# Moving work between engines in a two-layer graph-attention kernel: the adjacency mask, the inverse norms, the projections, and the writes of q and k in chunks

## The chip, the cores and the metric

The kernel runs on one core of a Trainium2 chip. The metric is the device time of one execution in microseconds. The core's engines each have an instruction stream of their own and wait for one another through semaphores: TensorE (PE, with its weight loads as PEld), VectorE (DVE), ScalarE (ACT), GpSimd (POOL) and SyncE (SP). In this kernel SP issues all transfers, which 16 DMA engines carry out.

## The reference

The inputs are `x` (3327 x 128) and a 0/1 adjacency `adj` (3327 x 3327, with ones on its diagonal). Two layers follow one another, and each ends in a residual and a layer norm.

```
# layer 0
norm2  = norm(x, axis=1)
cos    = beta * (x @ x.T) / (norm2 @ norm2.T + 1e-7)
P      = softmax(cos + (1 - adj) * -1e9)
x      = layernorm(x + P @ x)
# layer 1: 128 "d" groups of 8 features each
q, k, v = (x @ W.T).reshape(128, n, 8)   for Wq, Wk, Wv
a      = softmax(einsum('dnh,dmh->dnm', q, k) * 128**-0.5 + adj + adj)
out    = einsum('dnm,dmh->dnh', a, v).reshape(n, 1024) @ Wo.T
x      = layernorm(x + out)
```

The adjacency enters twice: as a mask in layer 0, and as an additive term (adj + adj) in layer 1, where the kernel needs it transposed.

## The kernel before

The 3327 nodes are padded to 3328 = 26 tiles (T) of 128 rows. There are four stages.

**Layer 0** (lines 175 to 447) runs in rounds t = -2 ... 27 of eight eighths k = 0 ... 7. The order of instructions on PE, ACT, DVE and POOL is the order in which the program calls them (`manual_schedule`); the order of transfers on SP is set by the framework's planner. A round works on several tiles at once:

- tile t: `scores` (L244), four pieces of 832 columns, at k = 0, 0, 2, 4. Each is two matmuls on PE (L190), a multiplication by the inverse norms `y` on DVE (L250) and an addition of the mask with a running minimum on DVE (L253).
- tile t+1: the inverse norms. `inverse_log` and `inverse_exp` (L228, L231) on ACT at k = 0 give a first estimate 1/(a+b) of `y`; `inverse_product` and `inverse_newton` (L236, L242) on DVE at k = 6 make one Newton step over all 3328 columns.
- tile t+2: `adj_chunk` (L209), seven chunks: up to four transposes on PE (L166) of the raw adjacency, a cast to bf16 on ACT (L215), and after the last chunk a write to `aT_s` in DRAM. At k = 7 `mask` (L221) turns the raw rows into (adj - 1) * 1e9 in place, on POOL.
- tile t+3: `load` (L199) at k = 5.
- tile t-1: `weights` (L269), two halves of Exp on ACT at k = 0; then at k = 1 ... 7 a chunk of `turn_weights` each (four transposes on PE, L166, and a copy out of PSUM on DVE, L280), followed one eighth later by `weigh0` (L288) on PE.
- tile t-2: `norm_begin`, `norm_root`, `norm_end` (DVE, ACT, DVE), `project_turn` at k = 3 (a transpose, and a copy to `x1T` on ACT, L332), and six halves of `project` (a matmul on PE, L342, and a copy to `row` on ACT, L343) at k = 4, 5, 5, 6, 7, 7. PSUM for `project` has one buffer, so a half's matmul waits for the copy of the half before it. Each second half issues the write of `row` to `q_s`, `k_s` or `v_s`.

**The preparation** (lines 746 to 804) has eight groups of 16 d. For k and for q, `prepare` loads a group (`nat`, 128 x 16 x 208, runs of 832 bytes), lets POOL reorder it into `by_t` (L754), turns it in seven chunks on PE, and splits each chunk into a high part (ACT, L765) and a low part (DVE, L766), which collect in two tiles of 3328 columns; a whole tile is then written to `kp_s` or `qp_s` in DRAM (L772). `prepare_values` does the like for v without the turn: `vals`, four sets of four d, is one tile and one write to `vt_s` (L786). From group 2 on, the first row maxima of the attention (`first_max`) run between. The tiles of units 0 and 1 are loaded after group 0.

**The steps** (lines 806 to 912) run over 288 units (a block of three query tiles times four d) of 26 steps each. A step uses `aT` (the adjacency of a block, turned, bf16) on PE (L633), and `eT` = exp(2 aT) on POOL (L860). The 26 tiles of `aT` of block 0 are loaded (`load_adj_tile`, L478) and turned into `eT` (`exp_adj_tile`, L485, on ACT) before the first step; those of later blocks within the steps. `aT`, `eT` and their pool `at_fix` are made after the preparation's pools are closed.

**The end** (lines 915 to 949) projects with Wo and makes the last layer norm.

Of the kernel before, what the change touches and what calls it, by code (L numbers as in the profile page):

```python
# [10 lines left out]
F32 = mybir.dt.float32  # L11
F32R = mybir.dt.float32r
# [7 lines left out]
P = 128  # L20
# [4 lines left out]
H = 8  # L25
# [21 lines left out]
def gnn_two_layers(  # L47
# [127 lines left out]
    with ExitStack() as l0:  # L175
# [42 lines left out]

        def mask(t: int):
            u = tiles[t]  # L220
            nc.gpsimd.tensor_scalar(u.raw, u.raw, -1.0, 1.0e9, op0=ALU.add, op1=ALU.mult)  # L221

# [4 lines left out]
            u.y = work.tile([P, NP], F32, name="y")  # L227
            nc.scalar.activation(u.y, norm_k, AF.Ln, bias=norm_c[:, t : t + 1])  # L228

        def inverse_exp(t: int):  # L230
            nc.scalar.activation(tiles[t].y, tiles[t].y, AF.Exp, scale=-1.0)  # L231

        def inverse_product(t: int):
            u = tiles[t]
            u.n = one_n.tile([P, NP], F32, name="n")
            nc.vector.scalar_tensor_tensor(  # L236
                u.n, norm_k, norm_c[:, t : t + 1], u.y, op0=ALU.add, op1=ALU.mult
            )

        def inverse_newton(t: int):  # L240
            u = tiles[t]
            nc.vector.scalar_tensor_tensor(u.y, u.n, -2.0, u.y, op0=ALU.add, op1=ALU.mult)  # L242

        def scores(t: int, j: int):  # L244
            u = tiles[t]
# [18 lines left out]
        def weights(t: int, i: int):  # L264
            u = tiles[t]
            if i == 0:
                u.den = small.tile([P, 2], F32, name="den0")
            part = u.s[:, i * half : (i + 1) * half]
            nc.scalar.activation(  # L269
                part, part, AF.Exp, bias=u.mn[:, NPC - 1 : NPC], scale=-1.0,  # L270
                accum_out=u.den[:, i : i + 1],
            )

        def turn_weights(t: int, c: int):
            u = tiles[t]
            if c == 0:
                u.pts = {}
            tp, a, b = turn(ps_tp, lambda k: u.s[:, k * P : (k + 1) * P], c)
            u.pts[c] = ptp.tile([P, 4, P], F32, name="pt")[:, : b - a, :], a, b
            nc.vector.tensor_copy(u.pts[c][0], tp)  # L280

        def weigh0(t: int, c: int):
            u = tiles[t]
# [65 lines left out]
        with tc.manual_schedule(  # L349
# [20 lines left out]
            )  # L370
            ones = const.tile([P, P], F32, name="ones")
            nc.gpsimd.memset(ones, 1.0)
            for t in range(3):
                load(t)
            ws = []
# [27 lines left out]
                nc.scalar.activation(piece(norm_k, j), score_piece(ones, sqT, j), AF.Sqrt)  # L403
            nc.scalar.preload_act_table_set("natural_log_exp_and_others")

            for t in range(-2, T + 2):

                def there(n: int):
                    return 0 <= n < T

                for k in range(8):
                    if k == 0 and there(t - 2):
                        norm_begin(t - 2)
                    if k == 0 and there(t - 1):
                        weights(t - 1, 0)
                        weights(t - 1, 1)
                    if k == 0 and there(t - 2):
                        norm_root(t - 2)
                    if there(t):
                        for i in {0: (0, 1), 2: (2,), 4: (3,)}.get(k, ()):  # L420
                            scores(t, i)
                    if k == 0 and there(t + 1):
                        inverse_log(t + 1)
                        inverse_exp(t + 1)
                    if k == 1 and there(t - 2):
                        norm_end(t - 2)
                    if k > 0 and there(t - 1):
                        turn_weights(t - 1, k - 1)
                        if k > 1:
                            weigh0(t - 1, k - 2)  # L430
                    if k == 3 and there(t - 2):
                        project_turn(t - 2)
                    if there(t + 2):
                        for i in {3: (0, 1), 4: (2,), 5: (3, 4), 6: (5,), 7: (6,)}.get(k, ()):
                            adj_chunk(t + 2, i)
                    if k == 5 and there(t + 3) and t >= 0:
                        load(t + 3)
                    if there(t - 2):
                        for i in {4: (0,), 5: (1, 2), 6: (3,), 7: (4, 5)}.get(k, ()):
                            project(t - 2, i)  # L440
                    if k == 6 and there(t + 1):
                        inverse_product(t + 1)
                        inverse_newton(t + 1)
                    if k == 7 and there(t + 2):
                        mask(t + 2)
                if there(t - 1):
                    weigh0(t - 1, NCH - 1)

# [6 lines left out]

    with ExitStack() as at:
        keys = at.enter_context(tc.tile_pool(name="at_k", bufs=3))
        sm = at.enter_context(tc.tile_pool(name="at_sm", bufs=2))
        ps_m = at.enter_context(tc.tile_pool(name="at_m", bufs=1, space=PSUM))

# [4 lines left out]
        for i in range(2):  # L465
            three = sm.tile([P, QT, 4, 32], BF16, name=f"parts{i}", bufs=1)
            nc.vector.memset(three, 0.0)
            parts.append(three)

        units = [(b, g) for b in range(NB) for g in range(G4)]  # L470
        NU = len(units)
# [246 lines left out]
        with tc.manual_schedule(  # L718
# [27 lines left out]
            with ExitStack() as pr:  # L746
# [3 lines left out]
                def prepare(g, src, dst):  # L750
                    nat = work.tile([P, HG, T * H], F32, name="nat")
                    nc.sync.dma_start(nat, heads(src)[g])
                    by_t = work.tile([P, T, P], F32, name="by_t")
                    nc.gpsimd.tensor_copy(  # L754
                        by_t.rearrange("p t (g h) -> p g t h", h=H),
                        nat.rearrange("p g (t h) -> p g t h", h=H),
                    )

                    high = work.tile([P, NP], F32R, name="high")
                    low = work.tile([P, NP], F32R, name="low")  # L760
                    for c in range(NCH):
                        tp, a, b = turn(ps_tp, lambda t: by_t[:, t], c)
                        cols = slice(a * P, b * P)
                        tp = tp.rearrange("p t k -> p (t k)")
                        nc.scalar.copy(high[:, cols], tp)  # L765
                        nc.vector.tensor_sub(low[:, cols], tp, high[:, cols].bitcast(F32))  # L766

                    for i, part in enumerate((high, low)):
                        nc.vector.tensor_copy(
                            part[:, NP - 1 : NP], part[:, NP - 1 - P : NP - P].bitcast(F32)  # L770
                        )
                        nc.sync.dma_start(  # L772
                            dst[g * HG : (g + 1) * HG, :, i].rearrange("d f n -> (d f) n"),
                            part.bitcast(F32),
                        )

                def prepare_values(g):
                    nat = work.tile([P, HG, T * H], F32, name="nat")
                    nc.sync.dma_start(nat, heads(v_s)[g])
                    vals = work.tile([P, HG, T, H + 1], F32, name="vals", bufs=1)  # L780
                    nc.gpsimd.memset(vals[:, :, :, H : H + 1], 1.0)
                    nc.gpsimd.tensor_copy(
                        vals[:, :, :, :H], nat.rearrange("p g (t h) -> p g t h", h=H)
                    )
                    nc.vector.tensor_scalar_mul(vals[:, :, T - 1], vals[:, :, T - 1], real)
                    nc.sync.dma_start(  # L786
                        vt_s[4 * g : 4 * g + 4].rearrange("a p h t f -> p a (h t f)"),
                        vals.rearrange("p (a h) t f -> p a (h t f)", a=4),
                    )

                k = 0
                for g in range(NG):
# [13 lines left out]
            fix = at.enter_context(tc.tile_pool(name="at_fix", bufs=1))  # L806
# [15 lines left out]
            aT = fix.tile([P, T, QB], BF16, name="aT1")  # L822
            eT = fix.tile([P, T, QB], F32, name="eT1")
            for j in range(T):
                load_adj_tile(0, j)

            def new_a():
                return [ps_a.tile([P, 512], F32, name="ea") for _ in range(2)]

# [4 lines left out]
            for j in range(T):  # L834
                exp_adj_tile(0, j)

            todo = []
            turn = []
# [149 lines left out]
```

## Time and profile before

Three runs took 16069.47, 16071.52 and 16073.84 us; the median is 16071.52. The profile is of one more execution:

| what | value |
|---|---|
| the profiled execution's own time | 16069.72 us |
| its span, first to last instruction | 16067.9 us |
| mean granted TensorE clock | 0.983 |
| busy: PE | 15521.0 us (97%) |
| busy: DVE | 13964.9 us (87%) |
| busy: ACT | 12606.0 us (78%) |
| busy: POOL | 13681.2 us (85%) |
| layer 0, to the last row of `v_s` issued | 0 to 1004.9 us |
| preparation, first `nat` load to the last landing | 1007.6 to 1316 us |
| steps, first to last | 1317 to 15951 us |
| end | to 16067.9 us |

How to read it: a group of instructions is named by line, engine, operation and what it writes and reads; "idle before" is the time for which its engine stood still just ahead of it, with what ended that; the chain of waits is followed back from the last instruction to what released each step. Shares of busy time are averages over stages with different limits, so each stage is read by itself. TensorE records two entries for one f32 matmul.

### The profile page before, as it was taken

To read this page: it belongs to the slowest core of one execution; us is meant where nothing else is said; L and a number is where in the kernel's file an instruction comes from. 1 tells how busy PE (TensorE), PEld (TensorE's weight loads), DVE (VectorE), ACT (ScalarE), POOL (GpSimd) and SP (SyncE) were. 2 spreads that over 40 slices of the span, in tenths; PEclk is the share of its full clock that TensorE was granted. 3 is DMA by queue.
4 is the path that set the end of the run, shared out by engine and by line. 5 is a ranking of instruction groups with operands and counts; after the bars stand their busy time and mean duration, and the time that the engine had idled before them with its cause. 6 is when DMAs were issued, how large, how long until landed. Compare 5 with 4: busy or idle time off the path is not lost.

```text
span 16067.9 us, 507030 instructions
## 1 busy us (share of the span) xinstructions
PE 15521.0 (97%) x217532; PEld 6936.2 (43%) x217532; DVE 13964.9 (87%) x16269; ACT 12606.0 (78%) x24826; POOL 13681.2 (85%) x9030
## 2 busy tenths in 40 slices
PE   6757999999999999999999999999999999999999
PEld 4543444444444444444444444444444444444555
DVE  6647999999999999999999999999999999998775
ACT  4426888888888888888888888888888888888776
POOL 1016999999999999999999999999999999998886
PEclk8878999999999999999999999999999999999999
DMA  3364111111111111111111111111111111111112
GB/s 128 117 231 145 45 50 51 54 47 51 51 51 50 51 46 55 51 51 45 57 50 45 49 53 54 44 50 51 51 50 51 50 52 51 51 45 60 61 61 75
DMA packets 483008, 995.72 MB, mean 62 GB/s; under 512 B 280274, under 2 KB 377424, under 8 KB 436208
## 3 DMA queue, kind: packets, MB, share of 16 engines
q1 hardware_dynamic: 480752, 963.28, 17.7%
q8 instruction: 1704, 27.92, 0.7%
q14 instruction: 552, 4.52, 0.1%
HBM read 813.16 MB, written 149.94 MB: 60 GB/s over the span
## 4 chain that ended last, share of the span: by engine, by line
PE 92%; DVE 5%; DMA 1%; ACT 0%; issue 0%; POOL 0%; SPq 0%; DVEq 0%; POOLq 0%; ACTq 0%
PE acc L663 28%; PE ea L633 20%; PE m L554 15%; PE eb L646 12%; PE ea L646 9%; PE eb L652 2%; PE ea L652 2%; DVE mx L569 1%; PE ea L619 1%; DVE y L242 1%; PE tp L166 1%; PE acc L288 1%; PE sc L190 1%; PE ea L681 1%; DVE mx L590 1%; DVE n L236 1%
## 5 line engine op out<-in xcount | busy, mean ns | idle before, releaser
L860 POOL TENSOR_TENSOR pb<-pb,eT 128x768 f32<-128x768 f32 (+1 forms) x7488 | 13186.4, 1767 | 1099.4 <-ACT pb L859 838.0
L569 DVE TENSOR_REDUCE mx<-m 128x2 f32<-128x1024 f32 x6784 | 8271.8, 1219 | 500.0 <-PE eb L652 278.6
L859 ACT ACTIVATE pb<-eb 128x768 f32<-128x768 f32 (+1 forms) x7488 | 5900.9, 788 | 2501.7 <-PE eb L652 1893.0
L554 PE MATMUL m<-kx,qx 32*128 32x512 f32 (+1 forms) x23296 | 6768.4, 470 | 56.1 <-DVE mx L569 49.3
L889 ACT ACTIVATE pa<-ea 128x384 f32<-128x384 f32 (+1 forms) x14976 | 6336.9, 477 | 53.5 <-PE ea L633 40.0
L663 PE MATMUL acc<-pa,vt 128*9 128x384 f32 (+1 forms) x29952 | 5902.5, 474 | 0.0
L663 PE MATMUL acc<-pb,vt 128*9 128x384 f32 (+1 forms) x29952 | 5900.5, 474 | 0.1
L590 DVE TENSOR_REDUCE mx<-m 128x1 f32<-128x512 f32 x6400 | 4377.5, 684 | 694.1 <-PE m L554 319.6
L646 PEld LDWEIGHTS <-one 3*128 3x128 bf16 x29952 | 1516.1, 91 | 5557.9 <-issue 4662.1
L633 PE MATMUL ea<-aT,two 128*32 128x384 bf16 (+1 forms) x59904 | 3714.8, 325 | 0.0
L652 PE MATMUL eb<-qx,kx 32*128 32x384 f32 (+1 forms) x14976 | 3473.2, 454 | 0.0
L652 PE MATMUL ea<-qx,kx 32*128 32x384 f32 (+1 forms) x14976 | 3443.6, 437 | 0.0
L646 PE MATMUL ea<-cx,one 3*128 3x384 bf16 (+1 forms) x14976 | 3297.9, 322 | 1.3
L554 PEld LDWEIGHTS m<-kx,qx 32*128 32x128 f32 x23296 | 2809.2, 182 | 404.1 <-DVE mx L569 97.4
L646 PE MATMUL eb<-cx,one 3*128 3x384 bf16 (+1 forms) x14976 | 2465.0, 326 | 15.2 <-ACT pb L859 14.4
L663 PEld LDWEIGHTS acc<-pa,vt 128*9 128x9 f32 x29952 | 1414.5, 91 | 784.5 <-issue 0.3
L633 PEld LDWEIGHTS <-two 128*32 128x32 bf16 x59904 | 945.3, 94 | 1420.2 <-issue 1280.9
L652 PEld LDWEIGHTS eb<-qx,kx 32*128 32x128 f32 x14976 | 1462.9, 189 | 0.0
L652 PEld LDWEIGHTS ea<-qx,kx 32*128 32x128 f32 x14976 | 1434.6, 182 | 8.2 <-issue 0.9
L663 PEld LDWEIGHTS acc<-pb,vt 128*9 128x9 f32 x29952 | 1410.2, 91 | 0.6 <-POOL pb L860 0.6
L594 DVE TENSOR_REDUCE mx<-m 128x2 f32<-128x512 f32 x1088 | 747.8, 687 | 96.4 <-PE eb L652 43.3
L118 POOL MEMSET raw<- 128x1 f32 x26 | 2.5, 100 | 509.6 <-DVE mn L253 509.6
(123 smaller groups left out, 5107.4 us busy)
## 6 DMA issues: line engine op xcount, KB each, us to landing
kx<-kp_s SPq DMA_DIRECT2D x576, 832.0 KB
vt<-vt_s SPq DMA_DIRECT2D x288, 468.0 KB
qx<-qp_s SPq DMA_DIRECT2D x1024, 48.0 KB
raw<-in_adj_dram SPq DMA_DIRECT2D x25, 1663.5 KB
aT_s<-aT SPq DMA_DIRECT2D x26, 832.0 KB
aT<-aT_s SPq DMA_DIRECT2D x208, 96.0 KB
vt_s<-vals SPq DMA_DIRECT2D x8, 1872.0 KB
q_s<-row SPq DMA_DIRECT2D x26, 512.0 KB
```

Of the source, the lines that this page charges most:

```text
L166: nc.tensor.transpose(tp[:, i, :], block(4 * c + i), ident)
L554: nc.tensor.matmul(dst, u.qx[rows(a), q * P : (q + 1) * P], u.kx[rows(a), k0:k1], start=True, stop=True,)
L569: nc.vector.tensor_reduce(u.mx[:, h, qs[0], c], m, axis=AX.X, op=ALU.max)
L590: nc.vector.tensor_reduce(u.mx[:, a, qs[0], c : c + 1], m, axis=AX.X, op=ALU.max)
L594: nc.vector.tensor_reduce(u.mx[:, a, qs[0] : qs[1] + 1, c], m.rearrange("p (q k) -> p q k", q=2), axis=AX.X, op=ALU.max,)
L633: nc.tensor.matmul(e[r, : u.nq], two[:, r], aT[:, j, : u.nq], start=False, stop=True, tile_position=(0, 32 * c), skip_group_check=True,)
L646: nc.tensor.matmul(e[:, : u.nq], one[r], u.cx[r, : u.nq], start=True, stop=False, skip_group_check=True)
L652: nc.tensor.matmul(e[:, : u.nq], u.kx[rows(a), j * P : (j + 1) * P], u.qx[rows(a), : u.nq], start=False, stop=stop, skip_group_check=True,)
L663: nc.tensor.matmul(acc[32 * h : 32 * h + H + 1, : u.nq], u.vt[:, h, j], pts[h // 2][:, h % 2, : u.nq], start=(j == 0), stop=(j == T - 1), ...
L859: nc.scalar.activation(pt_b[:, :, : u.nq], e_b[:, :, : u.nq], AF.Exp)
L860: nc.gpsimd.tensor_tensor(pt_b[:, :, : u.nq], pt_b[:, :, : u.nq], eT[:, j, : u.nq].unsqueeze(1).to_broadcast([P, 2, u.nq]), ALU.mult,)
L889: nc.scalar.activation(pt_a[:, h, : u.nq], e[:, : u.nq], AF.Exp)
```

## The change

In layer 0:

- `mask` goes from POOL to ACT, as Identity with a scale of 1e9 and a bias tile `minus` of -1e9, and from tile t+2 at k = 7 to tile t+1 at k = 0, after the inverse's Ln and Exp.
- The inverse's Exp, product and Newton step are cut into two halves of 1664 columns; the four DVE halves stand at k = 3, 4, 5, 6.
- The chunks 3 and 5 of `turn_weights` are copied out of PSUM by ACT instead of DVE.
- `adj_chunk` moves from k = 3 ... 7 to k = 4 ... 7, and `project` from six halves in k = 4 ... 7 to one half at each of k = 3 ... 7, and the sixth at k = 0 of the next round, ahead of everything else there. The loop has one more round for it.

In the preparation:

- The high and low parts are written chunk by chunk: tiles of 512 columns in four buffers, 14 writes for each `prepare` instead of two. `by_t` has one buffer instead of two.
- `vals` is one tile for each set of four d, in two buffers, with four writes instead of one.
- `at_fix`, `aT` and `eT` are made ahead of the preparation. The first block's adjacency tiles are loaded after group 0, in the program's text, and their exponentials follow groups 1 to 4, seven at a time.

In the built program's order on SP, 17 of those 26 loads stand among the last rows' writes of layer 0 and 9 after the loads of units 0 and 1; the loads of unit 2, which stood at the end of the preparation and after it, stand between groups 2 and 4.

```
-            nc.gpsimd.tensor_scalar(u.raw, u.raw, -1.0, 1.0e9, op0=ALU.add, op1=ALU.mult)
+            nc.scalar.activation(u.raw, u.raw, AF.Identity, bias=minus, scale=1.0e9)
...
-        def inverse_exp(t: int):
-            nc.scalar.activation(tiles[t].y, tiles[t].y, AF.Exp, scale=-1.0)
+        def part_of(i: int):
+            return slice(i * half, (i + 1) * half)
+
+        def inverse_exp(t: int, i: int):
+            y = tiles[t].y[:, part_of(i)]
+            nc.scalar.activation(y, y, AF.Exp, scale=-1.0)
...
-            nc.vector.tensor_copy(u.pts[c][0], tp)
+            if c in (3, 5):
+                nc.scalar.copy(u.pts[c][0], tp)
+            else:
+                nc.vector.tensor_copy(u.pts[c][0], tp)
...
-            for t in range(-2, T + 2):
+            for t in range(-2, T + 3):
...
+                    if k == 0 and there(t - 3):
+                        project(t - 3, 5)
...
                         inverse_log(t + 1)
-                        inverse_exp(t + 1)
+                        inverse_exp(t + 1, 0)
+                        inverse_exp(t + 1, 1)
+                        mask(t + 1)
...
+                    if there(t + 1):
+                        for step, i in {
+                            3: ((inverse_product, 0),),
+                            4: ((inverse_newton, 0),),
+                            5: ((inverse_product, 1),),
+                            6: ((inverse_newton, 1),),
+                        }.get(k, ()):
+                            step(t + 1, i)
                     if there(t + 2):
-                        for i in {3: (0, 1), 4: (2,), 5: (3, 4), 6: (5,), 7: (6,)}.get(k, ()):
+                        for i in {4: (0, 1), 5: (2, 3), 6: (4, 5), 7: (6,)}.get(k, ()):
                             adj_chunk(t + 2, i)
...
-                    if there(t - 2):
-                        for i in {4: (0,), 5: (1, 2), 6: (3,), 7: (4, 5)}.get(k, ()):
-                            project(t - 2, i)
-                    if k == 6 and there(t + 1):
-                        inverse_product(t + 1)
-                        inverse_newton(t + 1)
-                    if k == 7 and there(t + 2):
-                        mask(t + 2)
+                    if k > 2 and there(t - 2):
+                        project(t - 2, k - 3)
...
-                    by_t = work.tile([P, T, P], F32, name="by_t")
+                    by_t = work.tile([P, T, P], F32, name="by_t", bufs=1)
...
+                        high = work.tile([P, 512], F32R, name="high", bufs=4)[:, :n]
+                        low = work.tile([P, 512], F32R, name="low", bufs=4)[:, :n]
+                        nc.scalar.copy(high, tp)
+                        nc.vector.tensor_sub(low, tp, high.bitcast(F32))
+                        for i, part in enumerate((high, low)):
...
+                            nc.sync.dma_start(
+                                dst[g * HG : (g + 1) * HG, :, i, cols].rearrange(
+                                    "d f n -> (d f) n"
+                                ),
+                                part.bitcast(F32),
+                            )
...
+                    for q in range(HG // 4):
+                        vals = work.tile([P, 4, T, H + 1], F32, name="vals")
...
+                        nc.sync.dma_start(vt_s[4 * g + q], vals)
...
                         us[0], us[1] = load_unit(0), load_unit(1)
+                        for j in range(T):
+                            load_adj_tile(0, j)
+                    if 0 < g < 5:
+                        for j in range(7 * (g - 1), min(7 * g, T)):
+                            exp_adj_tile(0, j)
```

More of the change, by code (lines that the diff above doesn't have):

```diff
@@ L228, in inverse_log, with inverse_product, inverse_newton @@
             nc.scalar.activation(u.y, norm_k, AF.Ln, bias=norm_c[:, t : t + 1])
-        def inverse_exp(t: int):
-            nc.scalar.activation(tiles[t].y, tiles[t].y, AF.Exp, scale=-1.0)
-        def inverse_product(t: int):
+        def part_of(i: int):
[3 more added lines that the diff above has]
+            nc.scalar.activation(y, y, AF.Exp, scale=-1.0)
+        def inverse_product(t: int, i: int):
             u = tiles[t]
-            u.n = one_n.tile([P, NP], F32, name="n")
+            if i == 0:
+                u.n = one_n.tile([P, NP], F32, name="n")
+            h = part_of(i)
             nc.vector.scalar_tensor_tensor(
-                u.n, norm_k, norm_c[:, t : t + 1], u.y, op0=ALU.add, op1=ALU.mult
+                u.n[:, h], norm_k[:, h], norm_c[:, t : t + 1], u.y[:, h], op0=ALU.add, op1=ALU.mult
             )
-        def inverse_newton(t: int):
+        def inverse_newton(t: int, i: int):
             u = tiles[t]
-            nc.vector.scalar_tensor_tensor(u.y, u.n, -2.0, u.y, op0=ALU.add, op1=ALU.mult)
+            y = u.y[:, part_of(i)]
+            nc.vector.scalar_tensor_tensor(
+                y, u.n[:, part_of(i)], -2.0, y, op0=ALU.add, op1=ALU.mult
+            )
         def scores(t: int, j: int):
@@ L267, in weights @@
                 u.den = small.tile([P, 2], F32, name="den0")
-            part = u.s[:, i * half : (i + 1) * half]
+            part = u.s[:, part_of(i)]
             nc.scalar.activation(
@@ L372, in gnn_two_layers @@
             nc.gpsimd.memset(ones, 1.0)
+            minus = const.tile([P, 1], F32, name="minus")
+            nc.gpsimd.memset(minus, -1.0e9)
             for t in range(3):
@@ L457, in gnn_two_layers @@
         keys = at.enter_context(tc.tile_pool(name="at_k", bufs=3))
+        fix = at.enter_context(tc.tile_pool(name="at_fix", bufs=1))
         sm = at.enter_context(tc.tile_pool(name="at_sm", bufs=2))
@@ L468, in gnn_two_layers @@
             parts.append(three)
+        aT = fix.tile([P, T, QB], BF16, name="aT1")
+        eT = fix.tile([P, T, QB], F32, name="eT1")
         units = [(b, g) for b in range(NB) for g in range(G4)]
@@ L757, in prepare @@
                     )
-                    high = work.tile([P, NP], F32R, name="high")
-                    low = work.tile([P, NP], F32R, name="low")
                     for c in range(NCH):
                         tp, a, b = turn(ps_tp, lambda t: by_t[:, t], c)
+                        tp = tp.rearrange("p t k -> p (t k)")
                         cols = slice(a * P, b * P)
[L764 to L775, printed above, removed]
+                        n = (b - a) * P
+                        high = work.tile([P, 512], F32R, name="high", bufs=4)[:, :n]
[3 more added lines that the diff above has]
+                        for i, part in enumerate((high, low)):
+                            if b == T:
+                                nc.vector.tensor_copy(
+                                    part[:, n - 1 : n], part[:, n - 1 - P : n - P].bitcast(F32)
+                                )
+                            nc.sync.dma_start(
[3 more added lines that the diff above has]
+                                part.bitcast(F32),
+                            )
                 def prepare_values(g):
@@ L779, in prepare_values @@
                     nc.sync.dma_start(nat, heads(v_s)[g])
[L780 to L789, printed above, removed]
+                    for q in range(HG // 4):
+                        vals = work.tile([P, 4, T, H + 1], F32, name="vals")
+                        nc.gpsimd.memset(vals[:, :, :, H : H + 1], 1.0)
+                        nc.gpsimd.tensor_copy(
+                            vals[:, :, :, :H],
+                            nat[:, 4 * q : 4 * q + 4].rearrange("p g (t h) -> p g t h", h=H),
+                        )
+                        nc.vector.tensor_scalar_mul(vals[:, :, T - 1], vals[:, :, T - 1], real)
+                        nc.sync.dma_start(vt_s[4 * g + q], vals)
                 k = 0
@@ L804, in gnn_two_layers @@
                     k += 1
-            fix = at.enter_context(tc.tile_pool(name="at_fix", bufs=1))
             pp = at.enter_context(tc.tile_pool(name="at_p", bufs=4))
@@ L821, in gnn_two_layers @@
             )
[L822 to L825, printed above, removed]
             def new_a():
@@ L833, in gnn_two_layers @@
             nc.scalar.copy(us[0].cx, e[:, 0, :QB])
-            for j in range(T):
-                exp_adj_tile(0, j)
             todo = []
```

## The prediction

> **What bounds the kernel now.** I read the page first: the span, the busy shares and the chain that ended last, to see which stage each edit lies in.
>
> ```profile
> span 16067.9 us, 507030 instructions
> ...
> PE   6757999999999999999999999999999999999999
> ...
> POOL 1016999999999999999999999999999999998886
> PEclk8878999999999999999999999999999999999999
> DMA  3364111111111111111111111111111111111112
> ```
>
> A slice is 402 us. From the fifth slice on PE is over 90% busy: these are the attention steps, 1317 to 15951 us. None of their instructions changes, so their 14,630 us stay. The edits lie in slices 1 to 4: layer 0 (to 1007 us), the preparation of the parts of q, k and v (1007.6 to 1316 us), and the start of the steps.
>
> Layer 0 I read in the chain in order of time and in the timelines of one round (DVE, then POOL).
>
> ```profile
> 641.39 3.60 DVE n L236
> 645.02 6.26 DVE y L242
> 652.89 2.69 PE sc L190 x4
> 664.40 1.71 PE acc L288 x8
> ```
>
> ```profile
> 533.40 0.69 DVE L280 COPY pt<-tp 128x512 f32<-128x512 f32 x1 [4.30 <-PE tp L166]
> 534.01 3.68 DVE L236 SCALAR_TENSOR_TENSOR n<-norm_k,norm_c,y 128x3328 f32<-128x3328 f32 x1
> 537.72 6.26 DVE L242 SCALAR_TENSOR_TENSOR y<-n,y 128x3328 f32<-128x3328 f32 x1
> ```
>
> ```profile
> 537.00 3.51 POOL L221 TENSOR_SCALAR raw<-raw 128x3328 f32<-128x3328 f32 x1 [9.27 <-PE tp L166]
> ```
>
> A round starts with the reduction of `rden` (L295), at 111.4 us for t=2 and 902.8 us for t=24: 22 rounds of 35.97 us. In each, L236 and L242 stand undivided on DVE, 9.9 us, between the chunks of weights, and PE idles 4.8 us behind them (PE acc <- DVE rden). L242 takes 6.26 us under POOL's mask and 3.62 us in the first and last round, where no mask runs beside it. Before that PE ends things: DVE waits 3.75 and 4.30 us for L190 and L166. So DVE and PE take turns. ACT has 17.7 us of work in a round, POOL 3.7.
>
> The preparation I read in the DMA view of two stretches, one of `nat` loads and one of large writes:
>
> ```profile
> DMA packets 3480, 2.88 MB, mean 360 GB/s; under 512 B 18, under 2 KB 3480, under 8 KB 3480
> ```
>
> ```profile
> DMA packets 144, 1.70 MB, mean 426 GB/s; under 512 B 16, under 2 KB 16, under 8 KB 16
> ```
>
> These are 1120 to 1128 and 1064 to 1068 us. The 16 DMA engines are at a share of 1.0 from 1020 to 1316 us, but for some 8 us in all (the largest: 0.11 in 1256 to 1260). The stage is bound by transfers. The steps then start late (waits, 1004 to 1336 us, and ACT's timeline):
>
> ```profile
> PE eb L646 <- ACT pb L859: 14.4, 1, 14.4
> ```
>
> ```profile
> 1332.64 0.94 ACT L485 ACTIVATE eT<-aT 128x384 f32<-128x384 bf16 x2 [0.42 <-DMA aT<-aT_s]
> 1333.48 0.79 ACT L859 ACTIVATE pb<-eb 128x768 f32<-128x768 f32 x1
> ```
>
> The first exponential of a step stands behind 26 of L485, which wait for 26 loads issued only at 1316 us.
>
> **Layer 0, part by part.** DVE loses: L242 6.26 to 3.62 (no mask on POOL); two chunk copies, 2 x 0.64. L236 and L242 become four halves of 1.85, with other work between. DVE's busy time falls from 25.6 to 21.8 us.
>
> ACT gains the mask, two chunk copies (0.58 each, as L215's) and a split Exp. The mask on ACT is not in the trace; the nearest rows are 128x3328 Exp, 2.98, and Ln with a bias operand, 3.06; I bound it by 2.9 and 3.1 and take 3.0. A half Exp lies between half of 2.98 and the 1.67 of the weights' 128x1664: 1.57. ACT comes to 22.0 us.
>
> PE's work stays; I price it by start-to-start times in its timeline at 523 to 537 us: four transposes 0.45, four of L288 0.90, a projection half 0.86, a piece of scores 1.50. That is 22.9 us.
>
> No engine's sum is the round; the order is. The program's order puts the mask on ACT after Ln and both Exp, ahead of the copy of x1T (L332); PE's first projection half waits for x1T, and behind it on PE stand the fourth piece of scores and all later chunks. DVE waits for that piece, POOL for nothing. So a round is two legs in series.
>
> ACT's leg: last half's row 0.55, weights 3.43 (540.12 to 543.55), roots 0.35, Ln 3.09, two Exp 3.15, mask 3.0, x1T 0.3: 13.9 us. Beside it PE has only 8 us of work and DVE reaches the second chunk copy at 11.3 us, so PE's transpose of x1 is done some 2 us before ACT can take it.
>
> PE's leg, from the first half (eighth 3) to the sixth (next round): 5 halves 4.3, scores 1.5, weight chunks 3 to 6 1.6, seven adjacency chunks 2.9, L288 for chunks 2 to 6 4.05, 0.35 behind row 5's evacuation, 0.6 for a slow restart: 15.3 us. DVE has 8.7 us beside it (scores 2.1, three inverse halves 5.55, copies 1.05), so it hides; ACT has 8. With the copies of chunks 3 and 5 on ACT none is late. Then the sixth half itself, 1.05, moved past the next round's scores on PE and weights on ACT.
>
> Sum 13.9 + 15.3 + 1.05 = 30.3 us, 5.67 less than now. Bounds: without any restart loss and with every wait at its shortest 29.4; with 0.6 lost at three waits of PE and some 0.1 at each of ten hand-overs 32.4. I take 30.3, nearest to the rows.
>
> The restart: after 4.78 us of idling PE took 1.02 for the last two of L288 instead of 0.45, and after 2.31 us a group of four took 1.42 instead of 0.90, so a wait of 2.3 us costs some 0.5. The Trainium skill, "TensorE: Matmul & The Clock Gate", section "What's actually happening", says that the clock falls after at least one idle window of about 3.4 us; by it a wait of 2.5 us would cost nothing, and the time would be about 13 us lower. The row decides.
>
> Layer 0: 22 x 5.67 = 125 us. Round t=24 (31.1 us, no adjacency chunks) 3.5, t=25 1. Rounds before t=2: two L242 freed of the mask 5.3, one L253 (2.36 instead of 1.03) 1.3, an earlier start 1.4: 8. Together **-137 us**; rounds t=26 and 27 are serial projections of 2.76 us a half and stay.
>
> **Preparation and start.** Parts of q and k: 32 writes of 128 packets of 13,312 B become 224 writes, 28,672 packets of 2 KB (the last 1 KB). The large packets take 4 x 16 / 128 = 500 ns, 26.6 B/ns. The 832-byte packets take 8 x 16 / 3480 = 36.8 ns where that rate gives 31.3; by engine time (share 1.10) 40.5. So 5.5 to 9.2 ns a packet, times 24,576 more, over 16 engines: 8 to 14 us; I take 12. What else the chunks do lies between -8 us (every gap in the transfers filled, since writes start after one chunk, not seven) and +40: `by_t` now has one buffer, so each of 16 preparations has 3.0 us of POOL copy plus 1.8 us to its first chunk, against at most four chunks in flight, 2 MB or 5 us of transfers; if that cover is short by 2.5 us each, 40. I take 0: `nat` and `vt_s` transfers of the neighbouring group, 9 us and more, stand between.
>
> SP issues 192 more writes at 0.32 to 0.4 us: 70 us of 308 spread over it; hidden. The Trainium skill, "DMA: Bandwidth & Descriptors", section "Anatomy of one DMA", gives each transfer about 2 us of fixed cost, nearly all completion; paid one after another, 192 more would cost 384 us and the kernel would be near 16,320. The row speaks against that: 26 loads of 96 KB passed in 14.63 us, 0.56 each, so these costs overlap.
>
> First adjacency: in the built order 17 of 26 loads stand on SP among the last rows' writes of layer 0, where the DMA share is 0.1 to 0.2; 9 stand behind the loads of units 0 and 1 and ahead of group 1's `nat`: 9 x 0.5 = 4.5 us of a saturated queue, and 1 us on the path for the 17. Unit 2's loads are pulled in: 1.5 MB, 4 us. The 26 exponentials, 0.48 each, go in sevens behind groups 1 to 4 on ACT, which idles 25 to 37 us at a time there: hidden. At the end the wait goes: the steps begin at the last transfer instead of 17 us later (1316.1 to 1333.5). What is late next is that transfer, `vt_s`. Sum: +12 + 4.5 + 1 + 4 - 17 = **+5 us**, between -10 and +45.
>
> **Sum.** -137 + 5 = -132. From the profiled execution's 16069.7 (span 16067.9 and 1.8 around it): 15937.7. It lies 1.8 below the median of 16071.5, so 15940.
>
> **Rivals.** (a) The new ACT leg takes back most: PE starts each second half slow and x1T comes later still, so a round only loses what POOL's mask cost DVE, 2.64 us. For: ACT goes from 17.7 to 22.0 us and PE's idle time sits just ahead of its longest leg. Against: the work that L236 and L242 hid goes beside PE's leg. 22 x 2.64 + 8 = 66, with +5: 16010. (b) Slower: the chunk writes become bound by latency. In the built order each issue on SP waits for one of eight semaphores, so eight transfers are in flight, and four buffers of `high` and `low` allow no more. With a landing time L, 224 writes take 28 L. They now take 128 us (54.5 MB at 426 GB/s). L must be over 128/28 = 4.6 us to be felt and 9.6 us to eat 142 us. For: `nat` loads took 14 to 20 us to land in the chain, behind a full queue. Against: the 96 KB loads, eight at 0.56, took 4.5. At 12 us: 336 us, +208, and 16,135. (c) More: no restart loss and gaps filled, a round of 28.9: -156 - 12 - 10: 15,890.
>
> **Numbers.** Forecast 0.78, (a) 0.10, (b) 0.05, (c) 0.07. The forecast's bounds, 29.4 to 32.4 and -10 to +45, give 15,905 to 16,030 if taken together; one at a time 15,915 to 15,985. With (c)'s end the range is 15,895 to 16,000. 0.2% is 32 us, about what a measurement can tell from no change: faster 0.93, same 0.02 (the top of a), slower 0.05.
>
> **What would show it.** Right: L242 in halves of 1.85 with no POOL beside; rounds 30.3 us apart; PE's longest wait in a round on ACT x1T (2 to 3 us); the stage from the first `nat` load to the first step some 330 us, with the DMA share at 1.0; no wait of 14 us at the first step. Wrong: rounds near 33 (a), SP waiting for `kp_s` and `qp_s` landings with the share under 0.8 (b), or a change in the steps themselves, for which I see no reason.

## The result, and the profile after

The changed kernel takes 15986.99 us (median of 5 runs, 15984.42 to 15989.57) against 16071.52 before (5 runs, 16069.47 to 16073.84): a ratio of 0.9947, 95% interval 0.9933 to 0.9962. It is faster by 84.5 us; forecast were 132, and 15,940 us. The profiled execution took 15988.19 us, with a span of 15986.4 us, 81.5 less than before.

The span falls into three stages: layer 0 to the first load of `nat`, the preparation from there to the first exponential of a step (`pb`), and the steps with the end.

| us | before | after | difference | forecast |
|---|---|---|---|---|
| layer 0 | 1007.6 | 879.7 | -127.9 | -137 |
| preparation and start | 325.9 | 359.6 | +33.7 | +5 |
| steps and end | 14734.4 | 14747.2 | +12.7 | 0 |

The page of the kernel after, span and slices:

```profile
span 15986.4 us, 507863 instructions
...
POOL 0018999999999999999999999999999999998886
...
DMA  3382111111111111111111111111111111111112
```

POOL has nothing to do in the first two slices, now that the mask is gone, and the transfers reach their height in the third slice, no longer split over the third and fourth: layer 0 ends earlier.

**A round of layer 0.** ACT, in the kernel after (start, duration, instruction; in brackets the idle time ahead of it and what ended it), then DVE:

```profile
512.34 3.06 ACT L221 ACTIVATE raw<-raw,minus 128x3328 f32<-128x3328 f32 x1
515.30 0.24 ACT L344 COPY x1T<-pq 128x128 f32<-128x128 f32 x1
```

```profile
522.72 1.89 DVE L249 SCALAR_TENSOR_TENSOR y<-n,y 128x1664 f32<-128x1664 f32 x1
...
525.13 1.94 DVE L242 SCALAR_TENSOR_TENSOR n<-norm_k,norm_c,y 128x1664 f32<-128x1664 f32 x1
```

The mask costs ACT 3.06 us and stands right ahead of the copy of x1T, as forecast; the inverse's halves cost 1.89 and 1.94, with a chunk's copy between. But the rounds are not equal: their starts on DVE (L307) lie mostly 29.55 and some 32.0 us apart in turn (a few lie between, at 30.2 to 31.3), 30.80 on average from t=2 to t=24. TensorE's timeline of a short and of a long round:

```profile
486.04 1.13 PE L354 MATMUL pq<-wq,x1T 128*128 128x512 f32 x2 [1.71 <-ACT x1T L344]
487.00 1.56 PE L190 MATMUL sc<-xT 128*128 128x416 f32 x4
```

```profile
509.57 1.16 PE L300 MATMUL acc<-xn,pt 128*128 128x128 f32 x8 [2.31 <-DVE pt L292]
...
515.60 2.07 PE L354 MATMUL pq<-wq,x1T 128*128 128x512 f32 x2 [1.01 <-ACT x1T L344]
517.47 2.98 PE L190 MATMUL sc<-xT 128*128 128x416 f32 x4
```

After the shorter wait for x1T the same projection half takes 2.07 instead of 1.13 us and the same piece of scores 2.98 instead of 1.56: 0.94 + 1.42 = 2.36 us, nearly all of the 2.45 that the long round has more. The granted clock says why. Columns are the stretch, its length, TensorE's busy time in it, the clock, the DMA share and the rate:

```profile
476.60:480.01 3.41, 1.10 (x6) 1.00 0.00 0
480.01:483.42 3.41, 3.39 (x15) 0.50 0.07 22
483.42:486.83 3.41, 1.70 (x10) 1.00 0.00 0
...
507.32:510.73 3.41, 1.16 (x10) 1.00 0.06 19
510.73:514.14 3.41, 2.58 (x13) 0.50 0.00 0
...
517.56:520.97 3.41, 3.41 (x9) 0.50 0.00 0
```

In both rounds the 2.3 us for which TensorE waits for the first chunk of weights (`pt`) leave one stretch with a busy time of a third. The next stretch runs at half clock. In the short round it is filled and the clock is back after 3.41 us; in the long one it holds more waits, and the half clock lasts 10.24 us, into PE's leg with its first projection half and its piece of scores. The same view of all 205 such stretches from 100 to 800 us bears this out: the clock falls 23 times, 22 of them behind a stretch with 1.08 to 1.38 us of busy time, and no stretch that empty is followed by full clock.

**The preparation.** POOL's longest wait on a write in the kernel after (876 to 1240 us; total us, times, longest us), and POOL's timeline:

```profile
POOL vals L810 <- DMA vt_s<-vals: 116.1, 14, 19.0
```

```profile
1063.29 0.28 POOL L810 MEMSET vals<- 128x104 f32 x1 [17.46 <-DMA vt_s<-vals]
...
1064.67 0.88 POOL L811 COPY vals<-nat 128x832 f32<-128x832 f32 x1
1065.49 2.96 POOL L778 COPY by_t<-nat 128x3328 f32<-128x3328 f32 x1
```

`vals` has two buffers for four tiles of a group. The third waits until the first write to `vt_s` has landed; SP issues that write only after the 14 writes of `qp_s`; and the next group's `by_t` (L778), from which its chunks are turned, stands behind the third and fourth `vals` on POOL. DVE is a link of this loop too: its part of a `vals` tile (L815) must be done before the write, and from group 2 on it stands behind row maxima of the attention in DVE's order. Here the last write of `qp_s` is issued at 1054.91 us, and `vt_s` at 1060.64, right behind L815:

```profile
1059.78 0.68 DVE L618 TENSOR_REDUCE mx<-m 128x2 f32<-128x512 f32 x1
1060.37 0.38 DVE L815 TENSOR_SCALAR vals<-vals,real 128x36 f32<-128x36 f32 x2
```

SP has stood idle since 1057.1, after two loads of unit 2. So some 3.5 of the 17 us in which POOL stands still, with these loads 5.5, are not the 14 writes but DVE's order; no kernel with L815 ahead of the maxima was run. Meanwhile the transfers that POOL should feed run out, first around this wait, then over the whole stage (busy times of PE, PEld, DVE, ACT and POOL, then clock, DMA share and GB/s; the share adds up the times of packets, and can pass 1):

```profile
1055.00:1060.00 5.00, 2.77 (x8) 1.56 (x8) 4.41 (x6) 1.46 (x4) 0.00 (x0) 0.50 1.03 364
1060.00:1065.00 5.00, 0.00 (x0) 0.00 (x0) 1.00 (x4) 0.00 (x0) 1.47 (x4) 0.50 0.74 250
1065.00:1070.00 5.00, 1.50 (x7) 1.50 (x8) 2.90 (x1) 0.34 (x1) 3.45 (x2) 0.50 0.62 227
...
880.00:1240.00 360.00, 122.83 (x554) 92.64 (x555) 162.24 (x249) 74.05 (x141) 80.03 (x84) 0.59 0.95 331
```

Over the stage that is a share of 0.95 and 331 GB/s; before, the same view of 1008 to 1317 us gave 1.01 and 377. A stretch of nothing but chunk writes (900 to 905 us) moves 406 GB/s at a share of 1.06, against 426 for the large packets. At the first step:

```profile
1239.25 0.81 ACT L883 ACTIVATE pb<-eb 128x768 f32<-128x768 f32 x1 [1.93 <-DMA vt_s<-vals]
```

No exponential of L485's kind stands ahead of it any more: the steps begin 1.9 us after the last `vt_s`, as forecast.

**The steps** have no place where they lose: the distance from the first to the 241st copy to `ot` (one in each unit) is 12503.6 us before and 12518.5 after, 0.06 us a unit.

### The profile page after: what moved, and what is told of

Same layout as the page of the kernel before. It is cut to its first block, busy times and chain, and to the rows that moved or that the text cites. A ratio compares the mean times of both kernels' runs of the same rounds, so it can differ in the third digit from the quotient of the medians.

```text
span 15986.4 us, 507863 instructions
## 1 busy us (share of the span) xinstructions
PE 15512.6 (97%) x217532; PEld 6949.9 (43%) x217532; DVE 13908.2 (87%) x16293; ACT 12706.4 (79%) x24930; POOL 13584.2 (85%) x9053
## 4 chain that ended last, share of the span: by engine, by line
PE 92%; ACT 3%; DVE 2%; DMA 1%; issue 1%; POOL 0%; SPq 0%; ACTq 0%; DVEq 0%; POOLq 0%
PE acc L687 28%; PE ea L657 20%; PE m L578 15%; PE eb L670 12%; PE ea L670 9%; PE ea L676 2%; PE eb L676 2%; DVE mx L593 1%; PE ea L643 1%; PE pq L354 1%; PE tp L166 1%; DVE mx L614 1%; PE ea L705 1%; ACT pa L913 1%; PE acc L300 1%
```

## The experiments

Theory: layer 0 becomes shorter as forecast, but for stretches at half clock; the preparation becomes 30 us longer by the loop over `vals`; the steps' 12.7 us have a cause of their own. Rivals: the single `by_t` buffer, landings of the chunk writes, the early adjacency, the place of the tiles. Each kernel's time is a median, with its ratio to the kernel before on the same chip; the kernel before took 16069.37, 16072.04 and 16073.21 us beside the three sets.

### Layer 0 alone, and the preparation alone

`l0_only` is the changed layer 0 with all that follows as before; `prep_only` the reverse.

> The layer 0 part of the change alone; preparation and steps as before. Theory: the change is three separate sums in the traces, layer 0 -128 us, preparation and start +34, steps +12, and the first stands by itself: some 15,942 us, with the steps at 14,734 us from the first exponential to the end as before. Rival 1: the steps become slower because layer 0 ends earlier or runs differently (not because of the preparation's edits): 15,954. Rival 2: part of the preparation's loss comes from layer 0's new end (last rows later on the queue): the preparation from the first load to the last landing is longer than 309 us here too, by some us.

> The preparation part of the change alone (chunked writes, quartered vals, early adjacency), layer 0 as before. Theory: it loses by itself, +34 in preparation and start and +12 in the steps: some 16,117 us. Rival (the loss needs the new layer 0): the time stays near 16,071 to 16,085. If the steps are slow here (14,747 from the first exponential) the cause lies in where the preparation's edits put tiles or transfers; if they are 14,734, it lies in layer 0.

`l0_only`: 15954.81 us, ratio 0.9929 (0.9914 to 0.9943); layer 0 883.4, preparation 330.5, steps 14742.1. `prep_only`: 16103.81, ratio 1.0021 (1.0012 to 1.0031); 1005.6, 360.3, 14735.0. Alone, the preparation's edits make the kernel slower by 34 us, and the loss is all in the stage itself. The steps stay at 14,735 with them, although `at_fix` lies elsewhere: alone, the preparation's edits do not make the steps slower. Layer 0's edits do, by 7.7 us (the constant `minus` is among them, see below), with not one instruction of the steps changed: `l0_only` came out where its first rival stood, not at the theory's 15,942. Its preparation is 4.6 us longer than before, so a little of the second rival is there too.

### The loop over `vals`

```
-                        vals = work.tile([P, 4, T, H + 1], F32, name="vals")
+                        vals = work.tile([P, 4, T, H + 1], F32, name="vals", bufs=4)
```

> The changed kernel with four buffers of vals instead of two. Theory: the gaps in the transfers (some 33 us with a share below 1, against 8 before) come from a loop: GpSimd's third vals waits until the first vt_s write has landed, that write stands on SyncE behind 14 qp_s writes, and the next group's by_t copy stands behind vals on GpSimd. Four buffers break it: some 20 to 25 us less, 15,964, and the wait of vals on vt_s (116 us in the changed kernel) gone. Rival: by_t's single buffer makes the gaps: no change, 15,985 to 15,988. Rival 2: the transfers themselves take longer (packets of 2 KB), and gaps only move: -5 at most.

15955.51 us, ratio 0.9930 (0.9914 to 0.9947): 31.5 less than the changed kernel, more than the 20 to 25 expected. The preparation takes 328.6 us instead of 359.6. POOL's wait for `vt_s` is gone from the list, and the share is that of a full queue (same columns, 875 to 1205 us):

```profile
875.00:1205.00 330.00, 123.83 (x554) 93.32 (x555) 142.70 (x249) 73.88 (x141) 79.17 (x84) 0.60 1.02 359
```

The order on SP shifts with the buffers, too: the loads of unit 2, which the changed kernel has between groups 2 and 4, stand at the end again, most of them behind the last `vt_s`, and the profile puts the first step's wait down to one of them:

```profile
1204.27 0.81 ACT L883 ACTIVATE pb<-eb 128x768 f32<-128x768 f32 x1 [6.22 <-DMA qx<-qp_s]
```

So the 31 us are wait and order together, and what each is worth was not measured.

### A second buffer for `by_t`

The forecast's upper bound of +40 had the single `by_t` as its mechanism.

```
-                    by_t = work.tile([P, T, P], F32, name="by_t", bufs=1)
+                    by_t = work.tile([P, T, P], F32, name="by_t")
```

> The changed kernel with two buffers of by_t, as before the change. Theory (loop through vals): 0 to -5 us, 15,982 to 15,987. Rival (single by_t buffer, the mechanism bounded at +40 in the forecast): -20 to -25, 15,964.

15986.77 us, ratio 0.9948 (0.9933 to 0.9963), preparation 357.1: no difference that can be measured. POOL waits for `vt_s` as before (117.6 us, 14 times).

### The late adjacency

Four buffers for `vals`, and the first block's adjacency tiles made, loaded and exponentiated after the preparation, as in the kernel before.

> The changed kernel with four buffers for `vals` and with the first block's adjacency late, as in the kernel before; of the preparation's edits only the chunks are left. Theory (the forecast's terms hold once the loop over `vals` is cut: early loads cost 4.5 + 1 + 4 us and save 17 at the start): 7 us above the 15,955.5 of four buffers alone, 15,962. Rival (the early loads cost nothing): 15,972. Third (the start of the steps no longer waits 17 us with the chunks): 15,946 to 15,950.

15966.49 us, ratio 0.9934 (0.9919 to 0.9948), between theory and rival. The preparation takes 344.6 us, 16.0 more than with the early adjacency; ahead of its first step stand again, on SP,

```profile
1202.61 14.72 SPq L498 DMA_DIRECT2D aT<-aT_s  x26
```

and the last of the 26 exponentials ends about where the first `pb` starts, at 1219.83 us. So the early adjacency is worth 16 us net (forecast: 17 less 5.5, 11.5), and what is left of the edits, the chunks and the cut of `vals` into four, costs 344.6 - 325.9 = 18.7 (forecast for the chunks: 12). Unit 2's loads are not in it: with four buffers they stand at the end, as in the kernel before.

### The place of the tiles in SBUF

The constant `minus` stays allocated to the end and so may move all later tiles. `minus_big` makes it in a pool of layer 0:

```
-            minus = const.tile([P, 1], F32, name="minus")
+            minus = big.tile([P, 1], F32, name="minus")
```

`before_minus` adds the constant and its memset to the kernel before.

> The changed kernel with the bias tile `minus` made in a pool that is closed at the end of layer 0, so that everything made later stands where it stood in the kernel before. Theory (the 12.7 us that the steps take more come from where their tiles stand in SBUF, behind a constant that stays for good): steps back to 14,734 us, 15,974 us in all. Rival (they come from the altered instruction stream or from when layer 0 ends): steps stay at 14,747, 15,987.

> The kernel before with the constant tile `minus` added and filled, and used by nobody. Theory (place of the later tiles): steps 14,742 to 14,747 instead of 14,734, so 16,077 to 16,082. Rival (instruction stream or timing of layer 0): 16,069, as before.

`minus_big`: 15988.20 us, ratio 0.9947 (0.9932 to 0.9962): no gain in all; its steps take 14740.7, 6.4 less, its layer 0 and preparation 4.3 and 2.6 more. `before_minus`: 16077.68, ratio 1.0004 (0.9994 to 1.0013), 5.6 more than before in the same set; its steps take 14741.0. Half of the expected effect, in the expected direction both times; a later kernel, with the constant in its place, has 14732.0. The theory of the place falls as the sole cause.

### The mask out of ACT's leg

```
-                        mask(t + 1)
...
+                    if k in (4, 6) and there(t + 1):
+                        mask(t + 1, k // 2 - 2)
```

in halves of 1664 columns, while PE's leg runs.

> The changed kernel with the mask on ScalarE in two halves at eighths 4 and 6 instead of ahead of x1T. Theory (two legs in series, ACT's leg ends with the mask): TensorE's wait for x1T, 1.0 and 1.7 us in alternate rounds, falls to about 0.4, so 22 rounds lose 0.6 to 1.3 us: 15,958 to 15,974. Rival (rounds keep to the clock's windows: nine of 3.41 us are 30.7 us, the mean round now): the saving comes back as windows at half clock, 15,980 to 15,990, or the round falls by half a window at once, 22 x 1.7 = 37 us, 15,950.

15931.60 us, ratio 0.9912 (0.9896 to 0.9929), 55 less than the changed kernel: layer 0 takes 833.1 us, 46.6 less, and the steps 14737.7, 9.5 less. Rounds are 28.96 us on average (28.73 and 29.3 in turn). TensorE's wait for x1T is 0.35:

```profile
548.38 1.13 PE L354 MATMUL pq<-wq,x1T 128*128 128x512 f32 x2 [0.35 <-ACT x1T L344]
```

The saving of 1.84 us a round is more than the wait that went (0.66 and 1.36). The rest is clock: the half clock of 10.24 us in every second round has become one of 3.41. Clock and TensorE's busy time in the two rounds:

```profile
511.87:515.28 3.41, 1.09 (x9) 1.00 0.07 19
515.28:518.69 3.41, 3.14 (x16) 0.50 0.00 0
...
542.59:546.00 3.41, 1.60 (x12) 1.00 0.07 19
```

The same wait of 2.32 us for `pt` leaves 1.09 of one stretch busy in one round and, lying across two stretches, 1.60 in the next; only after the former is the clock halved: in the next stretch of the other round (2.29 busy) it is 1.00.

### TensorE kept busy while it waits

```
+        def keep_warm(t: int):
+            u = tiles[t]
+            u.turned = ps_x.tile([P, 512], F32, name="pq")
+            for _ in range(18):
+                nc.tensor.transpose(u.turned[:, P : 2 * P], ident, ident)
```

at k = 2, ahead of `weigh0`, and eight more ahead of the transpose of x1.

> The changed kernel with idle transposes of the unit matrix on TensorE, whose results nobody reads: 18 while it waits for the first chunk of weights (2.3 us in every round) and 8 ahead of the transpose of x1. Theory (a stretch of 3.41 us in which TensorE was busy for a third runs the next 3.41 or 10.2 us at half clock; that alone makes every second round 32.0 us instead of 29.5): no stretches at half clock in the rounds, all rounds near 29.5, 22 x 1.25 = 27 us less, 15,960. Rival (the clock falls for another reason than idling): still windows at half clock, 15,987, or up to 15,990 with the work added.

15948.33 us, ratio 0.9922 (0.9907 to 0.9937): 38.7 less, with 26 transposes more in each round. Layer 0 takes 846.8 us, 32.9 less (the preparation 2.8 and the steps 5.7 less); no stretch between 130 and 780 us is at half clock. A round of this kernel:

```profile
522.18 2.13 PE L343 MATMUL pq<-ident 128*128 128x128 f32 x18
...
530.69 1.13 PE L362 MATMUL pq<-wq,x1T 128*128 128x512 f32 x2 [1.17 <-ACT x1T L352]
531.65 1.56 PE L190 MATMUL sc<-xT 128*128 128x416 f32 x4
```

TensorE still waits for x1T, 1.17 us, and yet the projection half takes 1.13 and the scores 1.56. Most rounds are 29.56 us, the short round of the changed kernel (mean 29.61). The busy time and clock of the stretch behind one of 1.93 us busy:

```profile
498.00:501.41 3.41, 2.25 (x18) 1.00 0.02 5
```

So the long rounds come from the half clock, and that from TensorE's idling, whatever fills the time.

### The findings together

`late_mask_vals4` has the late mask and four buffers for `vals`; `late_mask_vals4_warm` adds the 18 idle transposes; `late_mask_vals4_hl6` has instead six buffers each for `high` and `low`.

> The changed kernel with the mask in two halves at eighths 4 and 6 and four buffers for `vals`. Theory (the two causes lie in different stages and add): 15,931.6 - 31.5 = 15,900. Rival (part of the 55 us of the late mask was chance in the steps, 9.5 us): 15,905 to 15,912.

> The same with 18 idle transposes in TensorE's wait for the first chunk of weights. Theory (with the late mask one window of 3.41 us in two rounds is at half clock, about 1.5 us of TensorE's time): 0.3 to 0.8 us less in a round, 7 to 18 us less than without them, 15,882 to 15,893. Rival (the first projection half then waits on ACT's leg all the same): no change against the kernel without them, 15,900.

> The changed kernel with the late mask, four buffers for `vals` and six instead of four for `high` and `low`. Theory (with the loop cut the transfers are the bound, at a share of 1.02): 0 to -5 us against four buffers, 15,895 to 15,900. Rival (ScalarE's and VectorE's waits for landings of kp_s and qp_s, 64 us in all, hold the stage up): 15 to 25 us less, 15,875 to 15,885.

`late_mask_vals4`: 15900.25 us, ratio 0.9892 (0.9878 to 0.9907), the forecast sum; 837.2, 327.4, 14732.0. With the idle transposes 15890.21, ratio 0.9886 (0.9869 to 0.9902), the fastest here and 97 us below the changed kernel: rounds of 28.73 us, layer 0 819.5, with a single stretch at half clock between 100 and 815 us, preparation 325.9; 12 of the 18 us that layer 0 gains are gone in the steps (14743.9).

`late_mask_vals4_hl6`: 15927.70, ratio 0.9909 (0.9894 to 0.9924): 27 us slower, where 0 to 25 less were expected; both theories fall. Its preparation takes 350.7 us, 23.3 more, at a share of 0.95, and its steps 9.5 more. ScalarE's wait for `kp_s` did fall, from 45.2 to 27.6 us. But with other buffers the planner gives SP another order. The writes of group 4 and the first loads of group 5 in both kernels, four buffers first:

```profile
1037.12 0.41 SPq L777 DMA_DIRECT2D nat<-k_s  x1
1042.13 3.08 SPq L817 DMA_DIRECT2D vt_s<-vals  x4
1045.26 1.17 SPq L777 DMA_DIRECT2D nat<-q_s  x1
```

```profile
1049.20 2.66 SPq L817 DMA_DIRECT2D vt_s<-vals  x4
1051.91 1.11 SPq L777 DMA_DIRECT2D nat<-k_s  x1
1053.08 3.06 SPq L777 DMA_DIRECT2D nat<-q_s  x1
```

With four, the next group's first load goes out before the `vt_s` writes; with six, behind them, and POOL's waits for `nat` of k rise from 261 to 318 us. That the order is the cause is read from these views; no kernel with six buffers and the old order was run.

## Why the prediction came out as it did

The direction and layer 0's mechanism were right, and the time lies within the range, but the centre was 47 us too low. In the spans it is 50.5: 9 in layer 0, 29 in the preparation, 13 in the steps. That the preparation stayed inside its bound of +45 is luck: what made it longer is not what the bound was worked out for.

- **Two legs in series: right.** In the long round shown, ACT's leg, from the last half's row (502.12) to the end of x1T (515.54), is 13.4 us (forecast 13.9), as in the short one. PE's leg with the sixth half is 29.55 - 13.4 = 16.1 in a short round (forecast 15.3 + 1.05). The mask on ACT is 3.06 (3.0), the halves 1.89 and 1.94 (1.85). Rival (a), ACT taking it all back, did not come, nor did the round of 28.9 of (c).
- **The restart: right in kind, too small.** Forecast were 0.6 us a round, so 29.7 without; without half clock the round is 29.61 (`warm`), with it 30.80: 1.2 us. The slow restart does not follow the length of the wait alone, as the forecast had it (some 0.5 us for 2.3): it depends on how a wait lies in the stretches of 3.41 us. 22 x 0.5 = 11 us are the miss of 9. The forecast named x1T as the longest wait; it is `pt`, 2.3 us, and it is the one that halves the clock. The Trainium skill, "TensorE: Matmul & The Clock Gate", section "What's actually happening", has the window of 3413 ns and says that it runs freely; the traces agree, every half clock shown above lasts one such window or three. Its rule that an idle window brings the clock down was weighed against the row and would have made a wait of 2.5 us free; the runs decide against that use of it, since windows in which TensorE was busy for 1.09 to 1.16 of 3.41 us were enough.
- **The rounds before t=2** gave 11.3 us (forecast 8), t=24 1.5 (3.5), and t=25 took 1.3 more (1 less).
- **"What else the chunks do ... I take 0": the step that failed.** The bound of +40 was near, its mechanism wrong: in `byt2` a second `by_t` changes nothing that can be measured, and in `vals4` two more buffers for `vals` take 31 us away, the wait and the changed order together. The change cut `vals` into four tiles in two buffers, and the prediction counted the writes on SP but did not follow POOL's queue: what is behind the waiting instruction there is the next group's `by_t`. The sentence "`nat` and `vt_s` transfers of the neighbouring group ... stand between" is what the loop undoes.
- **The other terms of the stage** nearly cancel as forecast: with the loop cut, the stage takes 2.7 us more than before, of chunks and cut `vals` +18.7 (chunks: 12) and early adjacency -16.0 (-11.5). The term of 4 us for unit 2's loads stays untested, since these go back to the end with the loop cut; without it the forecast is +0.5.
- **Rival (b), chunk writes bound by latency: no.** Landings of `kp_s` were 4.9 us and of `qp_s` 4.1 to 4.4, at the threshold of 4.6 and far from 9.6. The one kernel with more buffers for `high` and `low` has another order of transfers and does not decide it further. The section "Anatomy of one DMA" of the Trainium skill, "DMA: Bandwidth & Descriptors", which the prediction cites for 2 us a transfer, is written for transfers issued by GpSimd, and here SP issues them; no term of the sum used it.
- **The steps, "so their 14,630 us stay": off by 12.7 us.** Fourteen kernels with the same steps took 14,732 to 14,747 for them. It does not come with the preparation's edits alone (`prep_only` 14735.0); layer 0's edits alone bring 7.7 of it (`l0_only`); it is not the place of `minus` alone; and it runs on through the units. The cause stays open; 15 us is what the steps can scatter by from one build to the next, and the forecast had no term for it, though it names a change in the steps as a sign of being wrong.

## What to carry to other kernels

When a tile is cut into parts, go through the queue of every engine that fills it: with fewer buffers than parts, whatever stands behind the fill waits for a landing. In this layer a wait on TensorE is priced by the clock windows that it empties, not by its length alone: idle transposes in it took 1.2 us off each round without making the round's work less. Where a planner orders the transfers, a change of buffers is also a change of their order.

## What the runs showed of the hardware

- A stretch of 3.41 us in which TensorE was busy for 1.09 to 1.16 us was followed by half clock in each case shown; one with 1.60 or 1.70 was not. Over the changed kernel from 100 to 800 us, 22 falls of the clock followed 1.08 to 1.38 us of busy time and one followed 1.60; all other stretches with 1.59 or more kept it. In `l0_only`, one stretch with 1.41 kept it as well, so the limit lies somewhere between 1.38 and 1.60 and is not sharp in these figures.
- Where the next stretch was filled (3.14 and 3.39 us busy) the clock came back after it; where it held waits (2.58, then 2.40) the half clock stayed for three. Over the same 700 us it came back after 2.91 us or more and stayed at half after 2.79 or less.
- Rounds that alternate, long and short, look as if they kept step with these stretches: 30.80 us is near 9 of them (30.7), 28.96 near 8.5 (29.0). But `l0_only`, with the same layer 0 as the changed kernel, has 31.08 on average, so this is not shown.
- L242 of the kernel before took 6.26 us with POOL's mask beside it and 3.62 in the two rounds without it; with the mask on ACT its two halves took 1.89 each, 3.78 in all.
